# Times of their own for the steps of the last slots: a fused attention and deformable-convolution block on one Trainium2 core

## The chip, the cores and the metric

The kernel runs on one NeuronCore of a Trainium2 chip. The metric is the device time of one execution in microseconds (us); the median of three runs counts. Five engines work side by side, each through its own queue in order: TensorE (PE; its weight loads are shown as PEld), VectorE (DVE), ScalarE (ACT), GpSimd (POOL), and SyncE (SP), which here only issues DMAs. Semaphores make one engine wait for another.

## The reference

All values are float32. The input is `x` of 4 images of 64 x 64 pixels with 256 channels. Two layers follow each other.

```
# layer 0: self-attention over the 4096 pixels of an image
q, k, v = x @ wq + bq, x @ wk + bk, x @ wv + bv        # 32, 32 and 256 channels
x = gamma * (softmax(q @ k.T) @ v) + x
# layer 1: a DCNv3 block
h = ln(x)
p = h @ inproj_w + inproj_b                             # what is sampled
c = gelu(ln(depthwise_conv_3x3(h)))
offset, mask = c @ off_w + off_b, softmax(c @ mask_w + mask_b)   # 16 groups x 9 points
s = sum over the 9 points of mask * bilinear(p, point + offset)
x = x + s @ outproj_w + outproj_b
x = x + gelu(ln(x) @ fc1_w + fc1_b) @ fc2_w + fc2_b     # hidden width 1024
```

## The kernel before

**Tiles and slots.** The 16384 pixels are 64 units of 256 (4 rows of an image). The convolution of a unit needs the rows below it, so the second layer works on 65 tiles that are shifted by half a unit: tiles 0 and 64 have 128 pixels, the others 256. A *slot* is one round of the software pipeline. In slot s the attention of unit s runs; unit s-1 goes through `front` (end of the softmax, residual, layer norm, input projection), tile s-1 through `plan` (convolution, offsets, masks, bilinear weights), and tile s-2 through `sample` (the weighted sums over shifted rows) and `back` (output projection, layer norm, MLP, output). So the last attention is in slot 63, the last `front` in 64, the last `plan` in 65, and the last `sample` and `back` in 66.

**What the stages issue.**

- `attention` (L461): `e0` to `e3` are 16 matmul instructions each on PE (energies), `x0` to `x3` their exponentials on ACT, `w0` to `w15` eight matmul instructions each (L531: weights times values, into two accumulators). After the last of these, `w15` in the steady order, `front` reads the accumulators (`inverse`, L551).
- `plan` (L609): `tap0` on ACT, `tap1` to `tap8` on DVE (L635), `turn` (transposes on PE), `stats`, `shift`, `norm` (DVE with POOL, DVE, ACT), `turn2`, `gelu`, `heads0/1` (PE, L672), `bias0/1` (DVE), then on ACT and DVE `mask_exp`, `hat0` to `hat2`, `sums`, `invert`, `weigh`, `nearer`, `near`, `mask`, `product`, `y`, `x`, and `bounds` and `count`, whose results only the checks and the correction read.
- `sample` (L838): `rows` makes SP load a window of shifted rows (320 KB, L831; the pool has six buffers); `times` multiplies it by the weights (DVE, L851), `plus` adds up (L859), `across` sums over the columns (L864 to L868); the last `across` of a tile gives `sp`.
- `back` (L969, through `finish`, L884): `turn` (transposes of `sp`, PE), `copy` (ACT), `project_out` (PE, L904), `added` (DVE, L910), `stats`, `shift`, `norm`, `raised`, `turn2`, `scale`, eight `hidden` (PE, L928) each with a `gelu` (ACT, L936), `narrowed0/1` (PE, L945), `end` (DVE, L951) and the output DMA (L979).
- `far` (L1007): the correction for sampling points that lie further off than the windows reach: it picks points, gathers their pixels with indirect DMAs on POOL (`pair`, `point`, `rows`, `pixels`, `summed`), and sends one tile through the same `finish`. It runs once, near the end. `checks` compute on DVE and PE whether anything is left for the general code, which then would run in a loop after it; here that loop runs no round.

**What sets the order.** A table `WHEN` (L324) has one time for each step of each stage, in nominal us in a slot of T = 60. `whole` (L1130) collects the steps with slot x T + time, sorts them, and calls them in that order. Inside `manual_schedule` the four compute engines issue their instructions in the order of these calls. The DMAs of SP follow from it. The times in the table thus give an order, and no engine waits for a time. Waits come from the data and from buffers: a tile of a pool waits until a slot of the pool is free. The PSUM pool `ps` (L75) has two buffers for everything but energies and accumulators: transposes, projections, heads, `hidden` and `narrowed`. Pools with one buffer (`p1`) hold most of the tiles of `plan`.

Since every slot has the same times, the steps of the last slots are called in the order of the steady ones, although stage after stage drops out. A few steps show it: in slot 66, `far` has `turn` to `end` at 46.75 to 54.33, and `back` has `turn` of tile 64 at 54.71.

Of the kernel before, what the change touches and what calls it, by code (L numbers as in the profile page):

```python
# [16 lines left out]
def tile_attention_dcnv3_block(  # L17
# [259 lines left out]
    def shift(st, name, n=2):  # L277

        st["nm"] = sm.tile([P, 2], F32, tag="nm", name=f"nm_{name}")
        nc.vector.scalar_tensor_tensor(  # L280
            st["nm"][:, :n], st["mv"][:, :n, 0], -1.0, st["r"][:, :n], ALU.mult, ALU.mult
        )

    def normalised(st, srcs, name):
        nm = st["nm"]
        st["xn"] = xn = p1.tile([P, 2, C], F32, tag="xn", name=f"xn_{name}")
        for i, s in enumerate(srcs):
            nc.scalar.activation(  # L288
                xn[:, i, :], s, AF.Identity, bias=nm[:, i : i + 1], scale=st["r"][:, i : i + 1]
            )  # L290

    def scaled(pt, g, b, name, m=256):

        hT = p3.tile([P, C // P, 256], F32, tag="cT", name=f"hT_{name}")
        for k in range(C // P):
            nc.scalar.activation(  # L296
                hT[:, k, :m], pt[:, k, :m], AF.Identity, bias=b[:, k : k + 1], scale=g[:, k : k + 1]
            )
        return hT
# [5 lines left out]
    def ready(func):  # L305
        nc.scalar.activation(idle, minus_half[:, 0:1], func)
# [4 lines left out]
    def transposed(src, name, n=2, pool=None, tag="m"):  # L311

        pt = (pool or ps).tile([P, C // P, 256], F32, tag=tag, name=f"pt_{name}")
        for k in range(C // P):
            for i in range(n):
                nc.tensor.transpose(  # L316
                    pt[:, k, i * P : (i + 1) * P], src[:, i, k * P : (k + 1) * P], ident
                )
        return pt
# [3 lines left out]
    T = 60.0  # L323
    WHEN = {  # L324
        "first": {
            "load": -30.0, "turn": 0.0, "copy": 0.6, "keys": 4.3, "key_bias": 5.4, "values": 5.5,
            "value_bias": 7.4,
        },
        "project": {
            "load": -14.4, "turn": 19.72, "copy": 23.24, "values": 37.05, "value_bias": 42.74, "keys": 48.45,  # L330
            "key_bias": 50.49,
        },
# [50 lines left out]
        },  # L383
        "checks": {
            "range": 12.0, "left": 12.1, "largest": 12.2,
        },
    }

# [68 lines left out]
    def value_load(u):  # L457
        nc.sync.dma_start(V[u][:, :, :C], vd[u])
# [425 lines left out]
    def finish(x1, sp, name, n=2, after=None):  # L884
        m = n * P
        st = {}

        def parts():
            return [st["x1"][:, i, :] for i in range(n)]

        def turn():
            st["x1"] = x1() if callable(x1) else x1
            st["pt"] = transposed(sp() if callable(sp) else sp, f"s_{name}", n)

        def copy():
            pt = st["pt"]
            st["sT"] = p3.tile([P, C // P, 256], F32, tag="cT", name=f"sT_{name}")
            nc.scalar.copy(st["sT"][:, :, :m], pt[:, :, :m])

        def project_out():  # L900
            st["po"] = po = ps.tile([P, 2, C], F32, tag="m", name=f"pout_{name}")
            for i in range(n):
                for k in range(C // P):
                    nc.tensor.matmul(  # L904
                        po[:, i, :], lhsT=st["sT"][:, k, i * P : (i + 1) * P], rhs=ow[:, k, :],
                        start=(k == 0), stop=(k == 1),
                    )

        def added():
            nc.vector.tensor_add(st["x1"][:, :n, :], st["x1"][:, :n, :], st["po"][:, :n, :])  # L910

        def norm():
            normalised(st, parts(), f"b{name}")

        def raised():
            x1n = st["x1"][:, :n, :]
            nc.vector.tensor_add(x1n, x1n, f2b.unsqueeze(1).to_broadcast([P, n, C]))

        def turn2():
            st["pt"] = transposed(st["xn"], f"b_{name}", n)  # L920

        def scale():
            st["hT"] = scaled(st["pt"], g2, b2, f"b{name}", m)

        def hidden(c):
            st["ph", c] = ph = ps.tile([P, 256], F32, tag="m", name=f"ph_{name}_{c}")
            for k in range(C // P):
                nc.tensor.matmul(  # L928
                    ph[:, :m], lhsT=f1w[:, k, c * P : (c + 1) * P], rhs=st["hT"][:, k, :m],
                    start=(k == 0), stop=(k == 1),  # L930
                )

        def gelu(c):
            if c == 0:
                st["gT"] = gp.tile([P, NH, 256], F32, tag="gT", name=f"gT_{name}")
            nc.scalar.activation(  # L936
                st["gT"][:, c, :m], st["ph", c][:, :m], AF.Gelu, bias=f1b[:, c : c + 1]
            )

        def narrowed(i):  # L940
            if i == 0:
                st["pm"] = ps.tile([P, 2, C], F32, tag="m", name=f"pmlp_{name}")
            po = st["pm"][:, i, :]
            for c in range(NH):
                nc.tensor.matmul(  # L945
                    po, lhsT=st["gT"][:, c, i * P : (i + 1) * P], rhs=f2w[:, c, :],
                    start=(c == 0), stop=(c == NH - 1),
                )

        def end():  # L950
            nc.vector.tensor_add(st["x1"][:, :n, :], st["x1"][:, :n, :], st["pm"][:, :n, :])  # L951
            if after:
                after(st["x1"])

        d = {
            "turn": turn, "copy": copy, "project_out": project_out, "added": added,
            "stats": lambda: statistics(st, parts(), f"b{name}"),
            "shift": lambda: shift(st, f"b{name}", n), "norm": norm, "raised": raised,
            "turn2": turn2, "scale": scale,
        }  # L960
        for c in range(NH):
            d[f"hidden{c}"] = lambda c=c: hidden(c)
            d[f"gelu{c}"] = lambda c=c: gelu(c)
        for i in range(n):
            d[f"narrowed{i}"] = lambda i=i: narrowed(i)
        d["end"] = end
        return d
# [162 lines left out]
    def whole(general):  # L1130
        shifted.clear()
        wns, sps = {}, {}
        steps = []

        def put(slot, stage, some, later=0.0):
            for name, fn in some.items():
                steps.append((slot * T + WHEN[stage][name] + later, len(steps), fn))

        for b in range(B):
            for u in range(NU):  # L1140
                s = b * NU + u
                if b == 0:
                    put(-1, "first", project(b, u), 3.6 * u - 1.8 + WHEN["attention"]["e0"])
                else:
                    put(s - NU, "project", project(b, u))

                    i = u // 4 * 4 + u % 2 * 2
                    t = max(WHEN["attention"][f"w{j}"] for j in (i, i + 1))
                    steps.append(((NU * b - 1) * T + t + 0.5, len(steps), lambda u=u: value_load(u)))
                att = Attention(b, u, general)  # L1150
                some = att.steps()
                if general and u == 0:
                    put(s, "general", {"e0": some.pop("e0"), "x0": some.pop("x0")})
                put(s, "attention", some)
                put(s, "tables", {k: lambda f=f: ready(f) for k, f in TABLES.items()})
                put(s + 1, "front", front(att))
        for v in range(PN):
            put(v + 1, "plan", plan(v, wns, general))
            put(v + 2, "sample", sample(v, wns, sps))
            put(v + 2, "back", back(v, sps))  # L1160
        if not general:
            put(UN + 2, "far", far_round(UN - 3))
            put(UN + 2, "checks", checks)
            steps += [(3.5 * i - 55.0, len(steps) + i, fn) for i, fn in enumerate(loads)]
        steps.sort(key=lambda x: x[:2])
        with tc.manual_schedule(engines={nc.tensor.engine, nc.vector.engine, nc.scalar.engine, nc.gpsimd.engine}):
            for _, _, fn in steps:
                fn()
# [23 lines left out]
    def largest_of(n, name):  # L1192
# [12 lines left out]
    checks = {  # L1205
        "range": out_of_range, "left": any_left, "largest": lambda: todo.update(res=largest_of(2, "any")),
    }
# [44 lines left out]
```

## Time and profile before

| | |
|---|---|
| median of three runs | 3875.44 us (3873.26 to 3876.86) |
| profiled execution, its own time | 3876.21 us |
| its span | 3874.4 us |
| PE, DVE, ACT, POOL busy | 3777.5, 3424.4, 2204.0, 317.5 us |
| mean granted clock of PE | 0.987 |
| length of a steady slot late in the run | 55.18 us |
| end of the last attention | 3694.6 us |
| samples of tile 63, of tile 64 ready | 3801.7, 3833.4 us |

A row of the windows gives, for a stretch of the span, the busy time of each engine, the number of instructions in brackets, the granted clock of PE as a share of full speed, the share of the DMA engines and GB/s. A row of the timeline is start, length, engine, source line, operation, and output<-input tiles. A row of the waits says which engine waited for which, in total, how many times, and the longest. Busy time counts overlapping instructions of one engine once.

### The profile page before, as it was taken

The page shows a single profiled execution, that of the slowest core. Times are in us where ns is not written, and L with a number is a line of the kernel's source. Part 1 is how long each engine was busy: PE and PEld are TensorE (multiplying, and loading weights), DVE is VectorE, ACT ScalarE, POOL GpSimd, SP SyncE. Part 2 cuts the span into 40 slices and gives each one's busy share as a digit, 9 for nine tenths or more (in the row PEclk, how much of TensorE's full clock was granted, in tenths as well). Part 3 has the DMA queues.
Part 4 walks back from the last instruction along what each step waited for, and adds up shares of the span by engine and source line. Part 5 has one row for each costly group of instructions (what it writes and reads, how often), then busy time and mean ns, then how long its engine had stood idle before and what let it go on. Part 6 is the DMA issues. An engine that isn't in the chain of part 4 may idle for free.

```text
span 3874.4 us, 55924 instructions
## 1 busy us (share of the span) xinstructions
PE 3777.5 (97%) x20316; PEld 3125.1 (81%) x20316; DVE 3424.4 (88%) x6224; ACT 2204.0 (57%) x4262; POOL 317.5 (8%) x444
## 2 busy tenths in 40 slices
PE   8999999999999999999999999999999999999965
PEld 7788888888888888888888888888888888888844
DVE  2599899899999899899899899999999999999995
ACT  4556556556556556556556556556556556655632
POOL 1000000000000000000000000000000000000020
PEclk9999999999999999999999999999999999999977
DMA  5333333334343333333443333333433333233320
GB/s 149 90 103 88 93 104 89 93 102 133 94 121 90 94 101 90 95 100 95 134 120 90 96 98 92 96 96 94 120 106 107 91 92 93 82 94 90 88 77 25
DMA packets 231789, 378.02 MB, mean 98 GB/s; under 512 B 32880, under 2 KB 181936, under 8 KB 231504
## 3 DMA queue, kind: packets, MB, share of 16 engines
q1 hardware_dynamic: 221408, 367.46, 33.9%
q10 hardware_dynamic: 8512, 3.43, 0.4%
q8 instruction: 162, 2.65, 0.3%
q0 software_dynamic: 1584, 3.47, 0.3%
q14 instruction: 123, 1.01, 0.1%
HBM read 251.69 MB, written 122.56 MB: 97 GB/s over the span
## 4 chain that ended last, share of the span: by engine, by line
PE 94%; DVE 4%; DMA 1%; issue 0%; ACT 0%; POOL 0%; ACTq 0%; POOLq 0%; DVEq 0%
PE acc L531 46%; PE ph L928 11%; PE pmlp L945 11%; PE e L506 7%; PE po L672 5%; PE pout L904 3%; PE pv L438 3%; PE pp L588 3%; PE pkq L417 1%; DVE pw L851 1%; PE pt_s L316 1%; DVE pw L859 1%; PE pt_p L316 1%; PE pt_b L316 1%; PE pc L648 1%; PE pt_f L316 1%
## 5 line engine op out<-in xcount | busy, mean ns | idle before, releaser
L531 PE MATMUL acc<-V,ex 128*128 128x257 f32 x8192 | 1902.0, 382 | 0.1
L531 PEld LDWEIGHTS acc<-V,ex 128*128 128x128 f32 x8192 | 1532.4, 190 | 265.3 <-issue 66.2
L851 DVE TENSOR_TENSOR pw<-win,wn 128x1280 f32<-128x1280 f32 x640 | 931.9, 1482 | 8.1 <-ACT wn L795 1.4
L859 DVE TENSOR_TENSOR pw<-pw,pw 128x1280 f32<-128x1280 f32 x512 | 760.0, 1484 | 0.1
L519 ACT ACTIVATE ex<-e 128x512 f32<-128x512 f32 x1024 | 528.7, 603 | 49.6 <-PE e L506 47.4
L928 PE MATMUL ph<-hT_b,f1w 128*128 128x256 f32 (+1 forms) x2080 | 497.8, 383 | 4.2 <-ACT hT_b L296 2.5
L945 PE MATMUL pmlp<-f2w,gT 128*128 128x256 f32 x2048 | 466.4, 381 | 0.6 <-ACT gT L936 0.6
L928 PEld LDWEIGHTS ph<-hT_b,f1w 128*128 128x128 f32 x2080 | 387.1, 193 | 81.8 <-issue 19.9
L635 DVE SCALAR_TENSOR_TENSOR cv<-hs,dw,cv 128x256 f32<-128x256 f32 (+1 forms) x1076 | 427.6, 462 | 7.5 <-ACT cv L631 1.5
L945 PEld LDWEIGHTS pmlp<-f2w,gT 128*128 128x128 f32 x2048 | 386.6, 191 | 51.7 <-ACT gT L936 1.0
L288 ACT ACTIVATE xn_p<-pc,nm_p,rstd_p 128x256 f32<-128x256 f32 x128 | 65.4, 560 | 608.2 <-DVE nm_p L280 608.2
L936 ACT ACTIVATE gT<-ph,f1b 128x256 f32<-128x256 f32 (+1 forms) x520 | 236.2, 467 | 241.2 <-PE ph L928 240.0
L506 PE MATMUL e<-qs,kT 32*128 32x256 f32 x4096 | 295.7, 401 | 0.7 <-ACT ex L519 0.7
L519 ACT ACT_TABLE_LOAD x190 | 243.8, 1283 | 3.1
L506 PEld LDWEIGHTS e<-qs,kT 32*128 32x128 f32 x4096 | 186.2, 184 | 71.5 <-issue 63.6
L274 POOL TENSOR_SCALAR rstd_p<-mv_p 128x2 f32<-128x2 f32 (+1 forms) x65 | 80.4, 1237 | 1680.3 <-DVE mv_p L272 1680.2
L672 PE MATMUL po<-om_w,ge 128*128 128x432 f32 x512 | 200.1, 534 | 1.2 <-ACT ge L665 1.2
L761 DVE TENSOR_TENSOR pr<-hat 128x1296 f32<-128x1296 f32 x128 | 192.7, 1505 | 0.6 <-DVE nm_b L280 0.5
L936 ACT ACT_TABLE_LOAD x125 | 160.4, 1283 | 2.2
L665 ACT ACTIVATE ge<-pt_p,bd,gd 128x256 f32<-128x256 f32 (+1 forms) x130 | 65.9, 558 | 161.3 <-PE pt_p L316 161.3
L672 PEld LDWEIGHTS po<-om_w,ge 128*128 128x128 f32 x512 | 98.5, 193 | 72.8 <-issue 64.4
L681 DVE TENSOR_TENSOR om<-po,om_b 128x432 f32<-128x432 f32 x128 | 77.4, 604 | 88.2 <-PE po L672 88.2
(215 smaller groups left out, 3816.2 us busy)
## 6 DMA issues: line engine op xcount, KB each, us to landing
win<-xp SPq DMA_DIRECT2D x536, 320.0 KB, 4.1
omd<-om SPq DMA_DIRECT2D x63, 432.0 KB, 2.5
xs<-in_x_dram SPq DMA_DIRECT2D x64, 256.0 KB, 5.6
x<-in_x_dram SPq DMA_DIRECT2D x64, 256.0 KB, 2.7
x1d<-x SPq DMA_DIRECT2D x64, 256.0 KB, 3.2
xp<-xq SPq DMA_DIRECT2D x128, 128.0 KB, 2.4
x1b<-x1d SPq DMA_DIRECT2D x63, 256.0 KB, 2.8
spd<-sp SPq DMA_DIRECT2D x63, 256.0 KB, 2.1
```

The lines of the kernel that those rows point to most:

```text
L316: nc.tensor.transpose(pt[:, k, i * P : (i + 1) * P], src[:, i, k * P : (k + 1) * P], ident)
L506: nc.tensor.matmul(es[r][:, jj, :], lhsT=self.kT[2 * g + jj][rows4(r), :], rhs=self.qs[rows4(r), :], start=True, stop=not self.general,)
L519: nc.scalar.activation(ex, self.es[r], AF.Exp)
L531: nc.tensor.matmul(self.acc[i], lhsT=ex[:, jj, i * P : (i + 1) * P], rhs=V[t // 2][:, t % 2, :], start=(g == 0 and r == 0 and jj == 0), st ...
L635: nc.vector.scalar_tensor_tensor(dst, src, dw[:, k, j : j + 1], dst, ALU.mult, ALU.add)
L672: nc.tensor.matmul(st["po", i], lhsT=st["ge"][:, k, i * P : (i + 1) * P], rhs=om_w[:, k, :], start=(k == 0), stop=(k == 1),)
L761: nc.vector.tensor_mul(pr.rearrange("p a b c d g -> p a b (c d g)"), hat[:, :, i, 1, :].unsqueeze(1).to_broadcast([P, 3, 3, S]), hat[:, :, ...
L851: nc.vector.tensor_mul(st[r].rearrange("p d (g c) -> p (d g) c", c=GC), src.rearrange("p d (g c) -> p (d g) c", c=GC), wns[v][:, i, r] .re ...
L859: nc.vector.tensor_add(st[0], st[0], st[r])
L928: nc.tensor.matmul(ph[:, :m], lhsT=f1w[:, k, c * P : (c + 1) * P], rhs=st["hT"][:, k, :m], start=(k == 0), stop=(k == 1),)
L936: nc.scalar.activation(st["gT"][:, c, :m], st["ph", c][:, :m], AF.Gelu, bias=f1b[:, c : c + 1])
L945: nc.tensor.matmul(po, lhsT=st["gT"][:, c, i * P : (i + 1) * P], rhs=f2w[:, c, :], start=(c == 0), stop=(c == NH - 1),)
```

## The change

A second table `LATE` has times for the steps of single slots: attention 60 to 63, `front` 61 to 64, `plan` 60 to 65, `sample` 60 to 66, `back` 59 to 66, `tables` (loads of ACT's function tables) 60 to 63, `far` and `checks` in 66. `put` takes a step's time from it where there is one, and from `WHEN` otherwise. The times there run past the slot of 60, up to 875, so steps of different slots mix in a new order. The first 8970 of the 9806 calls stand as they were. No step is added or taken away. In `finish` the tile `x1` is looked up in `added`, where it is first used, and no longer in `turn`.

In the new order the attention steps of units 61 to 63 come earlier against the `hidden` and `narrowed` steps of tiles 58 to 60; `far` begins with `pair` behind attention 63's `w13` and its `finish` is spread between those of tiles 63 and 64; the `checks` and tile 64's `count` come during tile 64's `back`; most `rows` are called well before their `times`.

```diff
+    LATE = {
+        "attention": {
...
+            63: {"load": 45.22, "e0": 89.67, "x0": 91.49, "e1": 92.19, "w0": 98.07, "x1": 98.39, "w7": 99.54,
+                "w1": 104.93, "e2": 104.94, "w3": 106.18, "w4": 108.57, "w2": 110.23, "x2": 111.63,
+                "w9": 113.71, "e3": 117.35, "w11": 117.47, "x3": 117.74, "w12": 120.69, "w8": 121.81,
+                "w13": 124.71, "w14": 130.05, "w5": 130.64, "w6": 131.24, "w10": 133.48, "w15": 135.85},
+        },
...
+        "back": {
+            59: {"gelu3": 124.6, "narrowed0": 127.67, "narrowed1": 158.01, "end": 200.44},
...
+            65: {"load": 231.7, "turn": 283.37, "copy": 289.39, "project_out": 294.63, "added": 297.44,
+                "stats": 302.36, "shift": 313.92, "norm": 337.89, "turn2": 339.43, "scale": 342.52,
+                "hidden0": 344.19, "hidden1": 347.27, "gelu0": 348.97, "hidden2": 352.65, "gelu1": 353.4,
+                "hidden6": 353.54, "gelu2": 359.89, "raised": 361.19, "hidden3": 364.14, "gelu6": 365.47,
+                "gelu3": 368.06, "hidden7": 372.34, "gelu7": 382.47, "hidden5": 391.91, "gelu5": 394.03,
+                "hidden4": 398.07, "gelu4": 410.63, "narrowed0": 410.83, "narrowed1": 411.98, "end": 431.95},
+            66: {"load": 288.99, "turn": 387.66, "copy": 402.25, "project_out": 421.29, "added": 429.33,
+                "stats": 434.37, "shift": 445.1, "norm": 471.96, "turn2": 481.75, "scale": 507.88,
+                "raised": 509.75, "hidden0": 518.42, "hidden1": 521.83, "gelu0": 537.38, "hidden7": 544.77,
+                "gelu1": 592.54, "hidden6": 594.02, "gelu7": 597.18, "hidden2": 624.79, "gelu6": 640.13,
+                "gelu2": 683.98, "hidden5": 693.55, "hidden3": 694.32, "gelu5": 708.81, "gelu3": 730.03,
+                "hidden4": 845.87, "gelu4": 867.34, "narrowed0": 874.42, "end": 875.01},
+        },
...
+        "far": {
+            66: {"pair": -52.0, "point": -2.86, "rows": 1.1, "pixels": 28.14, "summed": 234.91,
+                "turn": 239.1, "copy": 240.93, "project_out": 244.79, "added": 245.23, "stats": 286.42,
+                "shift": 302.09, "norm": 313.82, "turn2": 351.07, "scale": 362.74, "hidden0": 363.41,
+                "gelu0": 367.91, "hidden1": 368.72, "gelu1": 373.72, "hidden7": 376.03, "gelu7": 378.88,
+                "hidden6": 382.55, "gelu6": 383.66, "hidden3": 384.49, "gelu3": 401.8, "hidden2": 404.53,
+                "raised": 447.38, "hidden5": 450.45, "gelu2": 454.93, "left": 456.08, "hidden4": 458.73,
+                "gelu4": 461.83, "gelu5": 461.84, "narrowed0": 478.58, "end": 490.63},
+        },
+        "checks": {
+            66: {"range": 395.84, "left": 485.76, "largest": 510.45},
+        },
+    }
...
         def turn():
-            st["x1"] = x1() if callable(x1) else x1
-            st["pt"] = transposed(sp() if callable(sp) else sp, f"s_{name}", n)
+            st["pt"] = transposed(sp(), f"s_{name}", n)
...
         def added():
+            st["x1"] = x1()
             nc.vector.tensor_add(st["x1"][:, :n, :], st["x1"][:, :n, :], st["po"][:, :n, :])
...
         def put(slot, stage, some, later=0.0):
+            late = LATE.get(stage, {}).get(slot, {})
             for name, fn in some.items():
-                steps.append((slot * T + WHEN[stage][name] + later, len(steps), fn))
+                when = late.get(name, WHEN[stage][name])
+                steps.append((slot * T + when + later, len(steps), fn))
```

## The prediction

> **What bounds the kernel now.** I read the page first: its totals and slices, then the same engines in five stretches, then the timeline of the last 75 us, then DVE's waits.
>
> ```profile
> PE 3777.5 (97%) x20316; PEld 3125.1 (81%) x20316; DVE 3424.4 (88%) x6224; ACT 2204.0 (57%) x4262; POOL 317.5 (8%) x444
> ...
> PE   8999999999999999999999999999999999999965
> ...
> DVE  2599899899999899899899899999999999999995
> ...
> PEclk9999999999999999999999999999999999999977
> ```
>
> PE is full until the last two slices (97 us each); there DVE is full and PE half empty at a lower clock. So two limits follow each other, and the change lies at their seam.
>
> ```profile
> 3494.00:3694.60 200.60, 199.93 (x1081) 165.42 (x1081) 189.32 (x339) 112.58 (x213) 16.38 (x22) 1.00 0.32 88
> 3694.60:3801.70 107.10, 56.76 (x187) 39.15 (x185) 100.20 (x221) 30.62 (x66) 24.49 (x21) 0.74 0.27 72
> 3801.70:3833.40 31.70, 24.05 (x89) 17.92 (x89) 23.69 (x47) 10.10 (x23) 1.17 (x2) 0.74 0.05 18
> 3833.40:3874.40 41.00, 22.38 (x106) 19.23 (x106) 4.60 (x14) 9.05 (x23) 2.68 (x5) 0.77 0.06 19
> 3529.06:3584.24 55.18, 55.18 (x302) 45.72 (x301) 52.19 (x94) 32.59 (x63) 4.40 (x6) 1.00 0.32 90
> ```
>
> The columns are window, length, then busy time of PE, PEld, DVE, ACT and POOL, then clock. The last row is a steady slot: 55.18 us, PE never idle, DVE 52.19. 3494.0 is where the two orders part; 3694.6 is the end of the last attention; 3801.7 and 3833.4 are the ends of sampling for tiles 63 and 64. DVE's idle time in the first four is 11.3, 6.9, 8.0 and 36.4 us: little to win in the first three, much in the last.
>
> ```profile
> 3801.28 0.41 DVE L868 TENSOR_TENSOR sp<-pw 128x256 f32<-128x256 f32 x1
> ...
> 3832.99 0.43 DVE L868 TENSOR_TENSOR sp<-pw 128x256 f32<-128x256 f32 x1
> ...
> 3838.19 6.12 PE L928 MATMUL ph_f<-hT_bf,f1w 128*128 128x128 f32 x32 [0.55 <-ACT hT_bf L296]
> ...
> 3844.14 3.71 PE L945 MATMUL pmlp_f<-f2w,gT_f 128*128 128x256 f32 x16
> ...
> 3847.69 0.38 PE L316 MATMUL pt_s<-ident,sp 128*128 128x128 f32 x2
> ...
> 3864.06 0.42 DVE L951 TENSOR_TENSOR x1b<-x1b,pmlp 128x256 f32<-128x256 f32 x1 [10.86 <-PE pmlp L945]
> ```
>
> The last tile's samples are ready at 3833.4, yet its transpose pt_s starts at 3847.7: in between the whole `far` chain goes through PE. From pt_s to the end it is another 26.7 us.
>
> ```profile
> DVE x1b L951 <- PE pmlp L945: 14.7, 5, 10.9
> DVE f_x_f L951 <- PE pmlp_f L945: 10.5, 1, 10.5
> DVE x1b L910 <- PE pout L904: 6.4, 5, 3.5
> ```
>
> (Total, times, longest.) DVE's longest waits are these two chains, one after the other.
>
> **The change, priced.** No instruction is added or removed. Each step's place is slot x 60 plus its entry; sorted so, the first 8970 of 9806 steps stand as before (up to slot 60's `w7`). The other 836 are reordered on PE, DVE, ACT, POOL and in SP's DMA order. I priced them from rows: `w` 1.73 (8 matmuls, chain of waits), `e` 1.1, hidden 0.87, narrowed 3.46, heads 1.45, project_out and project_in 1.73; on DVE times 1.46, plus 1.48, product 1.5, a pair of taps 0.81. They sum to 275 us on PE and 347 on DVE. DVE instructions overlap: my steady slot sums to 56.0 where 52.19 is measured, so DVE sums are taken x0.93 (323; the busy time from 3494 on is 317.8).
>
> *Attention forward, MLP back.* Before, PE has 197.7 us queued up to the last `w15` (3494 + 197.7 = 3691.7; it came at 3694.6, so sums serve). After, it has 169.9: 28 us of hidden, narrowed and their transposes go behind it. DVE has 172 us queued up to the `inverse` that waits for it. At each hand-over from PE to DVE I set the two sums side by side. Before, DVE arrives up to 8.7 us too soon (idle 11.3 measured). After, the worst is 6.0, at slot 62's `w15`; by the same ratio I take 8 us idle. PE's own hand-overs from DVE keep 2 to 17 us in hand until there; ACT (57% busy) and its table loads (24 changes between exp and gelu where there were 28, 1.28 us each, so -5.1 us) lie beside PE.
>
> *The DVE stretch up to tile 63's samples.* DVE work placed before them falls by 3.9 x 0.93 = 3.6 us (`left`, `bounds` and `summed` move behind, tile 64's masks before): 289.5 - 3.6 = 285.9. Waits there were 6.9 us. By the sums, round trips over PE and ACT mostly have other DVE work in front; short are bias1 and `end` of 60, `added` of 62 (project_out at a low clock, 3.79 for 1.92) and a shift behind POOL, 0.5 to 2 us each: 5 us, bounds 2 and 12. So tile 63 is sampled at 3494 + 285.9 + 8 + 5 = 3792.9 (before 3801.7).
>
> *Tile 63 to tile 64.* DVE has 25 us queued, with the `end` of 63 inside, behind that tile's full chain: transpose, copy and project_out 4 to 5 us, statistics and norm 5, hidden 7, narrowed 7, transposes 1 to 2. I take 28.5; bounds 25 and 31.7 (as before).
>
> *The last chain.* 26.7 us as measured from pt_s. Before the transpose and between it and project_out only two hidden steps of `far` remain (0.77 each, against a copy of 0.4); two more and a narrowed of 3.7 lie between project_out and turn2, where PE had 3.1 us idle: 3.3 us more. 30.0 instead of 41.0; bounds 26.7 and 36 (half the detour left). The checks go from 3817 to this chain: about 2.7 us of DVE and 0.6 of PE, which before lay in DVE's queue; now they stand in front of hidden0 while ACT scales (0.8), and cost 0.6 uncovered.
>
> *DMA queues.* The window loads (SP), before mostly listed with their use, go 10 to 90 nominal us ahead of it. SP works in order, and a load waiting for one of six buffers holds what is behind it; its longest such wait is 17.1 us. In the new order the step that frees the buffer always stands before the load, and x1b loads stand 13 us or more of DVE work ahead of `added`, against 2.8 us to land after 2.9 for the output that frees them: 0, or up to 17 once if that cover goes. That `x1()` is now read in `added` adds nothing; it only lets the load stand behind the transpose. `keep` of 63 (x1d store 3.2, reload 2.8) has 18 us. On POOL the gathers of `far` lose their haste: from `pixels` to `summed` 74 us of DVE instead of some 18, and the rsqrt steps stand ahead of them, where one waited 2.0 us: 0 to -2, I take 0.
>
> *New waits.* Tile 57's narrowed result is held until its `end` 30 us of DVE later, so PE has one of two PSUM buffers meanwhile. Nine allocations overtake an older tile in this way; behind each wait all later PE steps. Each at 0 (the next step needs the same release anyway) to 1.9 (a project_out). I take 0: heads1 waits for bias0 anyway, project_out for its copy.
>
> Sum: 3792.9 + 28.5 + 30.0 = 3851.4 against the span of 3874.4, so -23.0. The profiled execution took 3876.21, 0.8 above the median 3875.44; from the median, 3852.
>
> **A rule against it.** PE's clock was 1.00 up to 3715, 0.57 in the five us after (no matmul from 3713 to 3727) and 0.50 next; in the chain of waits eight po matmuls took 5.54 us at 3745 and 2.90 at 3513. The Trainium skill, "TensorE: Matmul & The Clock Gate", Part 1, says the same as a rule: half rate by default, and again after an idle window of some 3.4 us, full rate only after as long a busy one. Its section on oscillation shows a kernel that pays at every gap, which speaks against thinning PE's last 105 us over DVE's stretch. An estimate by that page: eight gaps, each with 3.4 us at half rate, cost 14 us, and the time would be 3866 if none were covered.
>
> **The rivals.** (a) *PE goes cold earlier*, while attention still runs, at tile 60's transpose, where it waits some 3 us. For: PE now has 170 us in 178. Against: 1.00 in all rows up to 3715, and PE is mostly behind DVE. A cold 20 us adds 10: 3862. (b) *`far` still stands in the last chain*: its gelu steps are on ACT in front of tile 64's norm, so the last chain stays 41: 3863. Against: its samples and gathers are done 20 us before. (c) *The other side*: the PSUM waits are real. Nine at 1.9 are 17 and leave a gain; slower by 0.2% needs 23 + 8 = 31, or 3.4 us at each of nine. For: PE is in order, and the readers that free a buffer are on DVE, which is the bound. Against: at most two such tiles are ever alive in the new order. At 4.2 each it gives 3890. (d) *Nothing*: the order is overruled by waits and DVE's total rules. DVE idle would have to stay at 62 us; 3874.
>
> **How the numbers follow.** Likeliest 0.70, on its own 3832 to 3866: below, DVE idles not at all (-13), then 25 and 26.7, so 3832; above, DVE waits as before (+5), 31.7 and 36. (a) 0.08, (b) 0.08, (d) 0.05, (c) 0.09. The measurement tells 0.2% (8 us) from no change, so faster is below 3868: 0.70 + 0.08 + 0.08 = 0.86; same 0.05; slower 0.09. The range 3836 to 3866 holds nearly all of the likeliest with (a) and (b).
>
> **What would show it.** Last `w15` near 3670 instead of 3694.6; tile 63's sp near 3793, tile 64's 28 us later; pt_s within 2 us of sp; DVE's 10.5 us wait for pmlp_f gone; DVE idle about 13 us up to tile 63. Wrong if PE waits for PSUM readers on DVE appear in the waits of 3494 to 3670, if a window load releases DVE's times steps, or if the clock falls under 1.00 before 3660.

## The result and the profile after

The changed kernel took 3846.75 us (median of four runs, 3846.41 to 3851.71). The kernel before took 3876.07 us beside it (3873.26 to 3876.86). The ratio is 0.9929, with a 95% interval of 0.9911 to 0.9946: 29.3 us, or 0.7%, faster. Measured again beside the experiments it was 3847.66 against 3874.49 us, ratio 0.9934 (0.9921 to 0.9948). The prediction was 3852 in a range of 3836 to 3866. The profiled execution took 3846.97 us, with a span of 3845.0. First the page of the kernel after: totals and slices.

```profile
PE 3770.7 (98%) x20316; PEld 3117.3 (81%) x20316; DVE 3421.7 (89%) x6224; ACT 2201.8 (57%) x4258; POOL 317.6 (8%) x444
...
PE   8999999999999999999999999999999999999977
...
DVE  2599899999999998998998998998999999999997
...
PEclk9999999999999999999999999999999999999979
```

The same work is done (20316 and 6224 instructions). The last two slices changed: PE from 6 and 5 tenths to 7 and 7, DVE's last from 5 to 7. The stretches of the kernel after, cut at the same events as before (last `w15`, samples of tiles 63 and 64 ready, end):

```profile
3494.00:3668.00 174.00, 171.51 (x926) 139.53 (x925) 165.35 (x301) 92.78 (x174) 18.38 (x21) 1.00 0.33 87
3668.00:3789.60 121.60, 84.09 (x319) 62.87 (x317) 116.85 (x241) 44.51 (x95) 21.26 (x21) 0.80 0.30 85
3789.60:3815.50 25.90, 21.25 (x102) 16.78 (x103) 23.92 (x49) 10.42 (x26) 2.95 (x5) 1.00 0.11 38
3815.50:3845.00 29.50, 18.89 (x96) 14.71 (x94) 5.79 (x24) 9.89 (x24) 1.89 (x3) 0.84 0.06 19
```

DVE's idle time is 8.65, 4.75, 2.0 and 23.7 us, where it was 11.3, 6.9, 8.0 and 36.4. PE's busy time in the second stretch rose from 56.8 to 84.1 us: the MLP steps that had stood in front of attention now run beside the sampling. The last attention ends some 26 us earlier, yet tile 63 is sampled only 12 us earlier (both with the 2.8 us that are set apart below), because DVE has nearly the same work to do up to there whatever PE does first.

The timeline of the last 56 us of the kernel after, DVE's and PE's rows:

```profile
3789.24 0.42 DVE L1064 TENSOR_TENSOR sp<-pw 128x256 f32<-128x256 f32 x1
...
3815.11 0.42 DVE L1064 TENSOR_TENSOR sp<-pw 128x256 f32<-128x256 f32 x1
...
3816.34 0.44 PE L316 MATMUL pt_s<-ident,sp 128*128 128x128 f32 x2
...
3821.60 5.41 PE L1141 MATMUL pmlp_f<-f2w,gT_f 128*128 128x256 f32 x16 [0.46 <-ACT gT_f L1132]
...
3828.12 4.72 PE L1124 MATMUL ph<-hT_b,f1w 128*128 128x128 f32 x32
...
3836.56 0.42 DVE L1147 TENSOR_TENSOR x1b<-x1b,pmlp 128x256 f32<-128x256 f32 x1 [7.75 <-PE pmlp L1141]
```

Tile 64's transpose `pt_s` starts 0.8 us after its samples are ready; before it was 14.3. DVE's waits in this end of the kernel after:

```profile
DVE x1b L1147 <- PE pmlp L1141: 7.7, 1, 7.7
DVE f_x_f L1147 <- PE pmlp_f L1141: 4.6, 1, 4.6
DVE x1b L1106 <- PE pout L1099: 1.5, 1, 1.5
```

The 10.5 us for `far`'s result are 4.6, and they lie beside tile 64's chain instead of in front of it.

**A difference that is not the change's.** The first 8970 calls are the same in both kernels, yet the `rg` of the first `front` starts at 106.39 us in the trace before and at 103.72 after, and the one near 3472 at 3474.68 and 3471.89: 2.8 us, of which 2.7 are there at the first `front`. Over all 14 profiled executions of this study that last mark lies between 3470.6 and 3474.7, also for kernels that differ in nothing before it, so it scatters. I take it as zero of time below; from it to the end the kernel before takes 399.7 us, the one after 373.1. The 26.6 us between are what the new order is worth in the traces; the other 2.8 of the profiles' 29.4 are not.

### The profile page after: what moved, and what is told of

Read it like the earlier page. It is cut to its first block, busy times and chain, and to the rows that moved or that the text cites. A ratio compares the mean times of both kernels' runs of the same rounds, so it can differ in the third digit from the quotient of the medians.

```text
span 3845.0 us, 55916 instructions
## 1 busy us (share of the span) xinstructions
PE 3770.7 (98%) x20316; PEld 3117.3 (81%) x20316; DVE 3421.7 (89%) x6224; ACT 2201.8 (57%) x4258; POOL 317.6 (8%) x444
## 5 line engine op out<-in xcount | busy, mean ns | idle before, releaser
L1124 PE MATMUL ph<-hT_b,f1w 128*128 128x256 f32 (+1 forms) x2080 | 498.8, 383 | 11.3 <-ACT gT L1132 7.5
L1124 PEld LDWEIGHTS ph<-hT_b,f1w 128*128 128x128 f32 x2080 | 384.5, 191 | 91.2 <-issue 15.5
```

Of the source, the lines that this page charges most:

```text
L1124: nc.tensor.matmul(ph[:, :m], lhsT=f1w[:, k, c * P : (c + 1) * P], rhs=st["hT"][:, k, :m], start=(k == 0), stop=(k == 1),)
```

## Experiments

Every time in the table is from the zero just named, in the profiled execution (last `w15`: end of its last matmul; samples and `pt_s`: start of the instruction). The last column is the median of all runs. The traces of e2 and e3 are of the shortest of their runs, 3859.0 and 3856.61 us, 4.7 and 2.9 us under the medians; the other traces lie within 2 us of theirs.

| kernel | last `w15` | samples 63 | samples 64 | `pt_s` of 64 | end | median us |
|---|---|---|---|---|---|---|
| before | 220.3 | 326.6 | 358.3 | 373.0 | 399.7 | 3876.07 |
| after | 196.4 | 317.3 | 343.2 | 344.5 | 373.1 | 3846.75 |
| e1 new, then old | 196.4 | 358.7 | 391.1 | 406.2 | 431.7 | 3905.12 |
| e9 e1, ends behind | 196.4 | 345.6 | 378.0 | 393.0 | 418.6 | 3892.91 |
| e2 old, then new | 220.3 | 328.1 | 357.7 | 358.9 | 385.1 | 3863.71 |
| e3 far in the way | 196.4 | 317.0 | 343.7 | 358.1 | 383.2 | 3859.53 |
| e4 far threaded only | 220.4 | 327.8 | 363.7 | 368.7 | 396.1 | 3870.39 |
| e5 windows at use | 196.4 | 317.3 | 343.1 | 344.3 | 373.4 | 3847.21 |
| e6 far early | 196.4 | 327.2 | 354.3 | 354.7 | 380.1 | 3855.16 |
| e7 kept warm | 196.4 | 317.0 | 342.9 | 344.1 | 371.7 | 3845.23 |
| e8 far early, warm | 196.4 | 328.6 | 356.5 | 356.9 | 381.8 | 3855.29 |
| e10 behind last samples | 196.4 | 317.1 | 341.5 | 346.2 | 373.3 | 3847.51 |
| e11 after, again | 196.4 | 316.9 | 342.8 | 344.0 | 373.1 | 3847.66 |
| e12 bounds behind | 196.4 | 317.2 | 342.8 | 344.1 | 371.3 | 3846.34 |

e6 and e8 differ in nothing up to tile 64's samples, and these stand 2.2 us apart; the kernel after was profiled twice and agrees within 0.4. So I read nothing into 2 us of one trace, unless it comes back in several.

### The two halves of the order: e1 and e2

The seam is the `inverse` of the last unit. e1 keeps the new order up to it and sorts the rest by the old times; e2 does the reverse. Each step carries its new time x[0] and its old one x[3]:

```diff
+        steps.sort(key=lambda x: (x[0], x[1]))            # e2: x[3]
+        cut = next(i for i, x in enumerate(steps) if x[4] == ("front", UN, "inverse")) + 1
+        steps = steps[:cut] + sorted(steps[cut:], key=lambda x: (x[3], x[1]))   # e2: x[0]
```

e1:

> The new order up to the inverse of the last unit (the steps in which attention of the last slots is moved forward and the MLP back), and from there on every step left sorted by its old time, with far's finish in one piece behind tile 64's norm. Theory (both parts count): the last w15 comes near 3670 and DVE keeps its lead, but the last chain, from tile 64's samples to the end, is the old detour of about 41 us again; without the new order of the tail the time is 3858 to 3866. Rival 1 (the gain is far's way out of the last chain and nothing else): 3871 to 3876, however early w15 is. Rival 2 (the gain is all in the attention part): about 3847.

e2:

> The old order up to the inverse of the last unit, and from there on the steps left in the new order. Theory: the last w15 stays near 3694 and DVE idles about 11 us before it, as before; after it the tail is the new one, with some 26 to 28 us from tile 63's to tile 64's samples and a last chain of 29 to 31 us: 3857 to 3863, that is 12 to 18 us of the 29. Rival 1 (far's detour is everything): about 3849. Rival 2 (attention is everything, the tail only fills what it is given): 3872 to 3876.

e1 took 3905.12 us (3903.33 to 3905.62), ratio 1.0073 (1.0056 to 1.009): slower than the kernel before. All three expectations miss. The last `w15` is as early as expected, but tile 63's samples come 32 us *later* than before. DVE's rows in e1 that carry long waits:

```profile
3684.49 0.69 DVE L1147 TENSOR_TENSOR x1b<-x1b,pmlp 128x512 f32<-128x512 f32 x1 [13.39 <-PE pmlp L1141]
...
3705.64 0.69 DVE L1147 TENSOR_TENSOR x1b<-x1b,pmlp 128x512 f32<-128x512 f32 x1 [18.33 <-PE pmlp L1141]
```

These are the `end` steps of tiles 59 and 60. The new order leaves their MLP for later, the old order of the rest puts it first, and DVE's `end` with it. DVE, which has the sampling of tile 61 and more to do, stands idle for 31.7 us behind two additions. Up to tile 64's samples it is idle for 59.4 us, in the kernel before for 26.3; these 33 us are all that the samples come later.

e2 took 3863.71 us (3859.0 to 3865.11), ratio 0.9967 (0.9955 to 0.998). That is 0.7 us over what I expected of its own theory, and far from both rivals. Up to tile 64's samples it is like the kernel before (357.7 against 358.3); its gain is the last chain, in the last row of its windows:

```profile
3692.27:3800.07 107.80, 54.36 (x185) 37.43 (x183) 97.15 (x209) 32.46 (x67) 18.58 (x20) 0.73 0.25 68
3800.07:3829.67 29.60, 25.02 (x99) 19.27 (x99) 23.86 (x47) 10.02 (x24) 2.82 (x5) 0.83 0.09 30
3829.67:3857.07 27.40, 17.30 (x97) 13.96 (x96) 6.13 (x24) 7.54 (x21) 1.88 (x3) 0.93 0.08 25
```

What follows: the two halves do not add up. In the traces the tail alone gives -14.6 us, the attention part alone +32.0, both together -26.6. With the new tail behind it the attention part is worth -12.0 in the traces, and by the medians 16 to 17 us, since e2's trace is of its shortest run. In the traces, from e2 to the kernel after, DVE's idle time up to tile 64's samples falls by 12.5 (27.9 to 15.5), its work up to there by 2.0, and the last chain grows by 2.5 (27.4 to 29.9): -12.0. Attention forward lets PE do the MLP under the sampling; it paid with the new tail behind it, where DVE's steps on the MLP's results stand further back too, and cost time with the old one.

### Is it the `end` steps? e9

```diff
+        ends = {("back", UN - 3, "end"): 3833.2, ("back", UN - 2, "end"): 3839.35}
-        steps = steps[:cut] + sorted(steps[cut:], key=lambda x: (x[3], x[1]))
+        steps = steps[:cut] + sorted(steps[cut:], key=lambda x: (ends.get(x[4], x[3]), x[1]))
```

> The new order of attention with the old tail once more, where DVE waited 13.4 and 18.3 us for the narrowed results of tiles 59 and 60; now the two end steps that wait stand behind DVE work that is ready (the end of tile 59 behind the rest of tile 61's sampling, that of tile 60 behind the masks and products of tile 62). Theory (the MLP was put back on PE, but DVE's step that reads its result was left where it was, and everything of DVE stands behind it): 8.8 us and some 6 to 11 us of DVE work come in front of the two waits, so 15 to 20 us of the 32 go, 3884 to 3892. Rival (PE's backlog itself decides, wherever DVE's steps stand): 3900 to 3906.

3892.91 us (3892.66 to 3894.74): 12.2 less than e1, just outside the range of the theory, and well below the rival's. The two waits are gone, but two others stand in their place:

```profile
3682.04 0.69 DVE L1113 TENSOR_TENSOR x1b<-x1b,f2b 128x512 f32<-128x512 f32 x1 [8.27 <-ACT xn_b L288]
...
3709.34 0.69 DVE L1106 TENSOR_TENSOR x1b<-x1b,pout 128x512 f32<-128x512 f32 x1 [14.38 <-PE pout L1099]
```

`raised` of tile 60 and `added` of tile 61 are the next DVE steps behind the same queue of PE and ACT: 22.7 us instead of 31.7. DVE's idle time up to tile 64's samples is 46.6 us, where e1 had 59.4. So the position of the `end` steps is a part of e1's loss that two moved steps show (12 of 32 us); that the rest has the same cause is what these rows say, but I did not move these steps too.

### `far` in the last chain: e3 and e4

e3 undoes one thing in the kernel after:

```diff
-                "turn": 239.1, "copy": 240.93, "project_out": 244.79, "added": 245.23, "stats": 286.42,
...
-                "gelu4": 461.83, "gelu5": 461.84, "narrowed0": 478.58, "end": 490.63},
+                "turn": 387.00, "copy": 387.02, "project_out": 387.04, "added": 387.06, "stats": 387.08,
...
+                "hidden7": 387.48, "gelu7": 387.50, "narrowed0": 387.52, "end": 387.54},
```

> The changed kernel with one thing undone: far's finish, from its transpose to its end, stands in one piece just before tile 64's transpose. Theory: PE's transpose pt_s of tile 64 waits again until far's hidden and narrowed steps are through, 10 to 14 us after the samples; the last chain is 38 to 42 us instead of 29.5 and the time 3855 to 3860. Since DVE is relieved of far's steps earlier, a part of it can come back. Rival (far's finish is hidden beside DVE's work wherever it stands): 3845 to 3849.

3859.53 us (3856.61 to 3860.09), as the theory had it: 10.1 us longer in the trace and 12.8 by the medians; of the 10.1, 9.6 lie after tile 64's samples. PE's rows in e3:

```profile
3819.77 6.41 PE L1119 MATMUL ph_f<-hT_bf,f1w 128*128 128x128 f32 x32 [0.55 <-ACT hT_bf L296]
3826.03 3.72 PE L1136 MATMUL pmlp_f<-f2w,gT_f 128*128 128x256 f32 x16
3829.59 0.38 PE L316 MATMUL pt_s<-ident,sp 128*128 128x128 f32 x2
```

e4 does that thing alone, in the kernel before:

```diff
-            "copy": 47.03, "project_out": 47.31, "added": 47.59, "stats": 47.87, "shift": 48.15,
...
-            "end": 54.33,
+            "turn": 18.0, "copy": 18.1, "project_out": 18.2, "added": 18.3, "stats": 18.4, "shift": 30.0,
+            "norm": 30.1, "turn2": 42.25, "scale": 42.3, "hidden0": 46.661, "gelu0": 46.662,
...
+            "raised": 46.76, "hidden5": 46.72, "hidden4": 46.73, "gelu4": 46.74, "gelu5": 46.741, "narrowed0": 46.8, "end": 46.9,
...
+    LAST = {
+        "turn": 46.671, "copy": 46.672, "project_out": 46.70, "added": 46.71, "stats": 46.715, "shift": 46.75,
+        "norm": 46.755, "turn2": 46.85, "scale": 46.86,
+    }
...
+                if (stage, slot) == ("back", UN + 2):
+                    when = LAST.get(name, when)
```

> The kernel before with one thing added: far's finish is threaded through the last tile's chain as in the changed kernel (its transpose to its scale earlier, two hidden steps before tile 64's transpose and two before its project_out, the rest with its narrowed between project_out and turn2). All else as before. Theory: the last chain is about 30 us instead of 41, everything ahead of it as before: 3863 to 3867. Rival 1 (with the old tail, DVE's steps of far are late and the chain keeps its length): 3872 to 3876. Rival 2 (all of the gain): about 3847.

3870.39 us (3868.39 to 3871.49), ratio 0.9987 (0.9977 to 0.9996): half of what I expected, and neither rival. The last chain did become shorter, 32.4 us from the samples instead of 41.4. But the samples themselves came 5.4 us later, mostly because `far`'s DVE steps now stood in front of them: 1.1 us more work between the samples of tiles 63 and 64, and a wait of 2.4 us for `pout_f` (the wait for tile 63's `pout`, 3.2 us, had been there before with 3.5). And tile 64's transpose still started 5.0 us after its samples, not 0.8. One step moved by itself brings its waits along; the new table moves what surrounds it as well.

### Window loads: e5

```diff
+                if late and stage == "sample" and name[:4] == "rows":
+                    when = late.get("times" + name[4:], WHEN[stage]["times" + name[4:]]) - 0.005
```

> The changed kernel, except that in the last slots each load of a window stands directly before the step that multiplies it, as the steady slots have it, and not 10 to 90 nominal us ahead. Theory: the order of PE and DVE carries the gain and the loads' lead only fills buffers that were landed in time anyway: 3845 to 3849, with no DVE wait on a window over 1 us. Rival (the lead of the loads is part of the gain): the times steps wait for their windows, 2 to 3 us each for some of them, and the time is 3851 to 3867.

3847.21 us (3846.42 to 3848.84), and every mark as in the kernel after: the early loads are no part of the gain.

### `far` out of the last chain: e6 and e8

```diff
-                "stats": 192.63, "shift": 209.09, "norm": 219.84, "turn2": 231.2, "scale": 248.48,
+                "stats": 192.63, "shift": 209.09, "norm": 219.84, "turn2": 231.2, "scale": 242.7,
...
-            66: {"pair": -52.0, "point": -2.86, "rows": 1.1, "pixels": 28.14, "summed": 234.91,
...
-                "gelu4": 461.83, "gelu5": 461.84, "narrowed0": 478.58, "end": 490.63},
+            66: {"pair": -52.0, "point": -2.86, "rows": 1.1, "pixels": 28.14, "summed": 45.3, "turn": 45.4,
+                "copy": 45.5, "project_out": 45.6, "added": 45.7, "stats": 45.8, "shift": 50.5, "norm": 51.3,
...
+                "gelu5": 62.93, "hidden7": 62.94, "gelu6": 62.95, "gelu7": 62.96, "narrowed0": 62.97, "end": 80.0,
```

`far`'s sum and finish then stand between the MLP of tiles 60 and 61, whose `scale` is called 5.8 nominal us earlier. e8 adds 26 transposes of the identity to it, at 422.0 of slot 66.

e6:

> The changed kernel with far's sum and finish moved out of the last chain altogether, between the MLP of tiles 60 and 61. Theory: the 5.4 us narrowed of far is gone from between tile 64's project_out and turn2, where PE has 3 us to spare, so the last chain is 26 to 28 us instead of 29.5; DVE's total is the same; 3843 to 3846, if tile 64's hidden steps do not run at a lower clock for it (then 1.8 us come back: 3845 to 3848). Rival (its gathers and its steps are now in the way earlier, and DVE waits for them or for PE): tile 63's samples come later than 3789.6 less the difference at the start, and the time is 3848 to 3856.

e8:

> far's finish between tiles 60 and 61, and 26 transposes of the identity on PE between tile 64's project_out and turn2, where PE would otherwise be idle; their result is not used. Theory: the last chain is free of far and runs at a clock of 1.00: 25 us instead of 29.5, and 3840 to 3844. Rival 1 (the clock falls all the same): the last chain 27 us and 3843 to 3847. Rival 2 (the transposes delay turn2): 3847 and over.

3855.16 us (3854.28 to 3858.32) and 3855.29 (3854.75 to 3856.35): e6's rival, slower than the kernel after by some 8 us. The last chain did fall to 25.8 and 25.3 us, as the theories had it; that e8's time fits its second rival is luck, since the transposes did not lengthen that chain. But tile 64's samples came 11 and 13 us later. The stretches of e6 between `w15`, the samples of 63 and those of 64:

```profile
3670.90:3801.70 130.80, 92.07 (x373) 69.75 (x371) 120.12 (x253) 48.96 (x107) 29.36 (x25) 0.83 0.28 79
3801.70:3828.80 27.10, 19.61 (x79) 15.35 (x79) 21.40 (x38) 7.79 (x19) 0.94 (x2) 0.87 0.08 28
```

DVE is idle for 10.7 and 5.7 us there (4.75 and 2.0 in the kernel after); a wait for `pout_f` (3.4) and waits of 1.9 each for `pmlp` of one tile and `pout` of another are the largest on PE. Four us won where DVE is idle anyway cost eleven where it is the bound.

### The clock in the last chain: e7, e10, e11 and e12

`far`'s narrowed took 5.41 us in the kernel after, where the prediction had 3.7. e7 adds 18 transposes around it:

```diff
+    WARM = (6, 8, 4)
+    WHEN["warm"] = {"warm0": 422.0, "warm1": 450.5, "warm2": 458.75}
...
+            for _ in range(n):
+                nc.tensor.transpose(st["t"], ident, ident)
```

> The changed kernel plus 18 transposes of the identity on PE into an unused PSUM tile, in the last chain (6 ahead of project_out's end, 8 and 4 among far's last hidden steps); their result is not used. Theory (far's narrowed took 5.41 us instead of 3.7 because the granted clock was 0.5 there, after PE had been busy for little over half of each us): the clock stays up, narrowed takes 3.7 and the time is 1 to 2 us less, 3844 to 3846. Rival 1 (the clock does not follow these gaps): the same, within 1 us, with the low clock in the same place. Rival 2 (the added transposes are in the way): 1 to 2 us more.

The windows around the start of that step in the kernel after (the clock is the first column behind the last bracket):

```profile
3819.00:3822.00 3.00, 1.70 (x10) 1.29 (x11) 1.74 (x9) 2.19 (x5) 0.81 (x2) 1.00 0.00 0
3822.00:3824.00 2.00, 2.00 (x7) 1.55 (x6) 0.40 (x3) 0.29 (x1) 0.00 (x0) 0.51 0.00 0
```

The windows of e7 at the same place:

```profile
3817.00:3820.00 3.00, 2.98 (x25) 2.44 (x23) 1.78 (x8) 2.17 (x5) 0.81 (x2) 1.00 0.00 0
3820.00:3822.00 2.00, 2.00 (x9) 1.79 (x10) 0.71 (x5) 0.68 (x2) 0.00 (x0) 1.00 0.00 0
```

In the kernel after PE was busy for 1.70 of 3 us, with no gap over 0.84, and the clock fell to 0.51. With the gaps filled it stayed at 1.00, and narrowed took 3.72 us. In three profiles without the transposes (the kernel after twice, and e5) the median matmul of that step took 505 to 521 ns, in three with them (e7, e10, e12) 379. e7 took 3845.23 us (3844.41 to 3845.9), e5 beside it 3847.21: as expected by the theory, though the intervals of their ratios overlap (0.9904 to 0.9934, and 0.9909 to 0.9939).

e10 is e7 with DVE work put behind tile 64's samples:

```diff
-                "y1": 168.86, "x_copies": 168.94, "x": 170.04, "count": 185.14, "bounds": 235.2},
+                "y1": 168.86, "x_copies": 168.94, "x": 170.04, "count": 185.14, "bounds": 622.0},
...
-                "count": 182.71, "y1": 185.59, "x_copies": 190.56, "x": 193.7, "bounds": 477.17},
+                "count": 182.71, "y1": 185.59, "x_copies": 190.56, "x": 193.7, "bounds": 562.01},
...
-                "bounds": 444.57},
+                "bounds": 502.02},
...
-                "x_copies": 348.43, "x": 348.45, "carry": 403.46, "bounds": 436.06, "count": 591.22},
+                "x_copies": 348.43, "x": 348.45, "carry": 403.46, "bounds": 442.03, "count": 591.22},
...
-                "hidden6": 353.54, "gelu2": 359.89, "raised": 361.19, "hidden3": 364.14, "gelu6": 365.47,
+                "hidden6": 353.54, "gelu2": 359.89, "raised": 440.4, "hidden3": 364.14, "gelu6": 365.47,
...
-                "hidden4": 398.07, "gelu4": 410.63, "narrowed0": 410.83, "narrowed1": 411.98, "end": 431.95},
+                "hidden4": 398.07, "gelu4": 410.63, "narrowed0": 410.83, "narrowed1": 411.98, "end": 440.5},
...
-            66: {"range": 395.84, "left": 485.76, "largest": 510.45},
+            66: {"range": 485.75, "left": 485.76, "largest": 510.45},
```

> The kernel with the 18 added transposes in the last chain (their result is not used), and with DVE work that tile 64's samples do not need put behind them: the bounds of four tiles (some 0.17 us each in DVE's queue), raised and end of tile 63 (0.6 us each), and the range check moved behind tile 64's norm. Theory (DVE is the bound up to tile 64's samples and has 23 us idle behind them): the samples come 1.5 to 1.9 us earlier and so does the end, 3843 to 3844. Rival (the later end of tile 63 holds its PSUM buffer and PE's hidden steps of far wait for it): the samples come earlier, the transpose does not, 3845 to 3847.

> The changed kernel as it is, beside the others on the same chip: 3845 to 3849 by all theories.

e10 took 3847.51 us (3845.61 to 3851.39), the kernel after beside it 3847.66 (3846.56 to 3852.6): nothing won. The samples came 1.3 us earlier than in the latter, the transpose 2.2 later, as the rival had it, but only partly for its reason. PE started tile 63's hidden steps at a low clock this time. In e10:

```profile
3800.00:3802.00 2.00, 1.93 (x5) 1.57 (x6) 1.19 (x1) 0.78 (x4) 0.17 (x1) 0.50 0.17 50
```

In the kernel after the same steps ran at 1.00 (3798.5 to 3800.5, 1.79 us busy). What differs is small: in all fourteen traces the clock changes only in steps of 3.41 us, and in the step before the low clock (3796.46 to 3799.87) PE was busy for 1.57 us in e10, while in the kernel after, where the same instructions came 0.3 us later from the zero, it was busy for 1.94 in the step around them (3794.73 to 3798.14). That made tile 63's narrowed 1.25 us late. Behind it `far`'s hidden steps waited once more for a gelu (0.46 us); that tile 63's late `end` held a PSUM buffer then is argued from the order, no row names it.

e12 keeps `raised` and `end` where the kernel after has them:

> The kernel with the 18 added transposes in the last chain (their result is not used), with the bounds of four tiles and the range check behind tile 64's samples, but raised and end of tile 63 where the changed kernel has them. Theory (it was the late end of tile 63 that kept far's hidden steps from PSUM): far's hidden steps run as early as in the changed kernel, the samples come 0.5 to 0.7 us earlier; since PE came to the transpose 0.8 us after the samples anyway, little of it reaches the end: 3844 to 3846, 1 to 3 us under the changed kernel, all from the clock. Rival (the moved bounds themselves disturb the last chain): 3847 and over.

3846.34 us (3845.68 to 3851.12), just over the expected 3844 to 3846 and under the rival's 3847. `far`'s hidden steps are early again and the last chain has its full clock (371.3 to the end, the shortest of all), but the moved bounds brought no more than 0.4 us at the samples, and the time is not told apart from that of the kernel after. So e7 and e12 are 1.4 and 1.8 us shorter than the kernel after from the zero to the end, with the reason in the rows; in the runs this lies within the scatter.

## Why the prediction was right

**By its steps.** Set against the kernel before from the zero mark, it had -8.8 us at tile 63's samples, -3.2 to tile 64's and -11.0 for the last chain, -23.0 in all. The traces have -9.3, -5.8 and -11.5: -26.6.

- *Attention forward.* Last `w15` predicted near 3670, measured 3668.3 (the common start moves it by 2.8). DVE idle predicted 8 us, measured 8.65. Right.
- *The DVE stretch to tile 63.* 5 us of idle predicted, 4.75 measured; DVE's work fell by 4.5 us where 3.6 was predicted. Right, and the reason is the one given: DVE is the bound, so only its idle time and its work count. 24 us of earlier attention became 9.
- *Tile 63 to tile 64.* This term was mis-sized: 28.5 us predicted, 25.9 measured, of 23.9 work and 2.0 idle. I had left 3.5 us of tile 63's chain uncovered; it was covered nearly to the end, at a clock of 1.00 where it had been 0.74 before.
- *The last chain.* 30.0 predicted, 29.5 measured, with two errors that cancel: `far`'s narrowed took 5.41 us instead of 3.7 (clock 0.51), and tile 64's hidden steps ran at 1.00 behind it, in 4.72 us, where they had a clock of 0.50 at their start before (3854 to 3858) and took 6.51. That the sum came out is luck. The working also names 0.6 us for the checks that its 30.0 does not hold; in the trace the wait of tile 64's first hidden step behind its transposes grew by 0.35 us (0.90 where it was 0.55). e3 shows the detour's price directly (10.1 in the trace).
- *DMA queues, window loads:* priced at 0, and 0 by e5. *New PSUM waits:* priced at 0; PE's waits from 3494 to 3668 add up to 2.4 us (1.5 for exponentials, 0.9 for samples), none for a buffer. Behind 3668 there are four waits that the kernel before has not:

```profile
PE ph L1124 <- DVE x1b L1147: 0.8, 1, 0.8
PE pt_s_f L316 <- DVE x1b L1106: 0.8, 1, 0.8
PE ph L1124 <- DVE x1b L1106: 0.8, 1, 0.8
...
PE ph_f L1124 <- DVE x1b L1106: 0.5, 1, 0.5
```

None of these PE steps reads what the additions write; the additions read a PSUM result and so free its buffer. These are the waits that were priced at 0: 2.9 us on PE, three of the four while DVE is the bound. What they cost in time no run shows by itself.

**The rivals.** (a) PE going cold early: the clock is 1.00 up to 3680. (b) `far` still in the last chain: refuted by the transpose 0.8 us after the samples; e3 is what it would have been, 3859.5 where I had 3863. (c) PSUM waits: none before 3668, 2.9 us in all behind it, far from the 31 that this rival needed. (d) Nothing: refuted.

**The rule weighed against the change.** From the Trainium skill, "TensorE: Matmul & The Clock Gate", Part 1, I had worked out an estimate of 14 us for eight gaps. PE did run at low clocks, 0.70 from 3680 to 3760, but DVE had only 4.75 us idle in the whole stretch, so at most that much of it reached the path up to tile 63's samples. In the last chain the price was 1.4 to 1.8 us by e7 and e12. The page's section "A second HAM failure mode: psum-queue depth-cycling" tells of short idles between groups of matmuls that make the clock swing; the row 3819 to 3822 agrees with it. The idle window of some 3.4 us that the rule of Part 1 names is not there: in the 3 us before the fall the longest gap is 0.84. (The eight `po` matmuls that the prediction compares take 5.53 and 3.06 us in the timeline's rows, not 5.54 and 2.90; the argument stands.)

**What is missing.** The prediction's mechanism was right in each of its three stretches, though the number of the last came out by luck. What it did not say is that the parts need each other: I priced attention and tail as a sum, and e1 shows that the first alone would have made the kernel slower by 29 us. The median lies 5.3 us under the prediction. In the profiled executions the difference is 6.4 us (29.4 against 23.0): 2.8 of the start's scatter, 2.6 of the tile 63 to 64 term, and 0.5 each of the other two.

## What to carry to other kernels

When a step of one engine is put back in an order written by hand, look at the steps of the bounding engine that read its result: left where they were, they make the bounding engine wait, and all that stands behind them too. The same move was worth -12 us in the traces with the new order of the tail and +32 with the old one; moving two of the readers alone (e9) took back 12 of the 32, and the rest was not taken apart. Moving an engine's work earlier is worth what idle time it takes from the engine that is the bound, not the distance it moved (24 us earlier, 9 gained). And a side task that must pass through the last chain is best threaded into the gaps there; taken out of it and put where the bound is, at the one place that was tried, it cost more (e6) than it had in the chain.

## What the runs showed of the hardware

- The granted clock fell to 0.51 without any long gap: PE was busy for 1.70 of the 3 us ahead of it, longest gap 0.84 (kernel after, 3819 to 3822), while in e8 a gap of 2.35 us behind dense matmuls left it at 1.00 (3826 to 3828).
- 18 small transposes of the identity, 2.46 us in all, in the idle slots of PE kept the clock at 1.00 and shortened a step of 16 matmuls from 5.41 to 3.72 us.
- The same instructions at the same place ran at 1.00 in one execution and at 0.50 in another (tile 63's hidden steps, the kernel after and e10). The clock changes in steps of 3.41 us in all fourteen traces, and PE had been busy for 1.94 and for 1.57 us of the step before: a shift of the instructions by 0.3 us was enough. These steps took 7.20 and 8.74 us.
- The same first steps end up to 4 us apart between executions (zero mark at 3470.6 to 3474.7), which is more than the smaller effects here. Comparing marks from a common step inside the trace takes it out.
